# Symmetric attention scores of layers 2 and 3: computed from the diagonal on, the rest by transposition

## The chip, the cores and the metric

The kernel runs on one core of a Trainium2 chip. The metric is the device time of one execution in microseconds (us), the median of several runs. Times within an execution come from the hardware profiler's trace of one of them.

## What is computed

The reference takes node features `x` (16 batches, 1024 nodes, 128 features) and a symmetric 0/1 adjacency matrix `adj` (16 x 1024 x 1024) with ones on its diagonal. Four graph layers follow each other, and each ends with `x = layernorm(x + layer(x))`. Layer 0 has batch norms over all batches. Layer 1 is an attention with additive scores. Layers 2 and 3, which the change touches, have this form; since `adj` is 0 or 1, only `a_0` counts:

```python
def scores(a):
    return leaky_relu(einsum('bnd,bmd->bnm', h * a, h), negative_slope=0.2)
alpha = full(adj.shape, -9e15)
for k, a in enumerate((a_0, a_1, a_2, a_3)):
    alpha = where(adj == k + 1, scores(a), alpha)
alpha = softmax(alpha, axis=-1)
return einsum('bnm,bmd->bnd', alpha, h)
```

The score of nodes n and m is the sum over d of `a[d] * h[n, d] * h[m, d]`, so the score matrix is symmetric, and so is the masked one, as `adj` is symmetric.

## The kernel before

Everything below is in `fast_path`; a `general_path` stands behind it for inputs that fail some tests, and these do not take it. A first part, up to about 390 us, does layer 0 over all batches, since its batch norms need sums over all of them. The rest, which the change touches, does layers 1 to 3 batch by batch. P is 128, N is 1024, D is 128, C = N / P = 8 row chunks, H = G = 2 halves of 512 columns, and A is D + 1.

A `Batch` object has one method for each stage. `weights` (L862) makes row chunk c (128 rows, 1024 columns) of the score matrix of layer 2 or 3. Two matmuls (L867) of 512 columns each, with the chunk of `xw` (the transposed features times `a_0`) as the stationary operand and `xt` (the transposed features) as the moving one, fill a PSUM tile `pbig` of two banks. VectorE subtracts a penalty `pen` from it, which is large where there is no edge (L870), and applies the leaky relu (L871). ScalarE takes the exponential in place (L872). The result is `e`, one tile of 8 x 1024 columns for each layer, with one buffer.

`sum` (L874) multiplies `e` with the features of the layer's input, to which a column of ones is joined, so that the column D of the product is the softmax's denominator. For an output chunk c it runs over m: the stationary operand is the block `e[:, m, c*P:(c+1)*P]`, that is row chunk m and column chunk c (L880), and the product accumulates in a PSUM tile `pacc` that holds up to three output chunks. Three such calls make a layer's sums. VectorE then divides, adds the residual (L888) and collects the layer norm's moments (L722, L723). `apply` (L742) ends the layer norm on ScalarE.

Other stages of a batch: `transpose` (L757 to L761) makes `xt` and `xw`; `residual0` does layer 0's last step (L777, L784, L786, L789); `scores1` (L804 to L806) makes two exponentials of one row for layer 1; `chunk1` does layer 1's row chunks (penalty L827, a comparison of `adj` with its transpose from the diagonal on L835, weights L838 and L841, matmuls into `po` L848). The PSUM tiles come from three pools of eight banks together: `r_big` with 2 buffers of two banks, `r_sum` with one of two banks, `r_acc` with 2 of one bank. Operands in fp32 are multiplied in two passes, so a matmul shows as two instructions in the trace; a transpose shows as one.

The order of the work is written out by hand. `place` (L927) gives each step of a stage a position: a whole number for the turn, plus a fraction that runs from a first to a last value over the stage's steps. In one turn t four batches are in work: layer 1 of batch t, layer 2 of t - 1, layer 3's scores of t - 2 and its sums of t - 3:

```python
for t in range(-1, B + 3):
    place(t, 0.04, 0.92, t, layer1)
    place(t, 0.08, 0.50, t - 1, scores, 2, V_L2)
    place(t, 0.54, 0.94, t - 1, sums_of, 2)
    place(t, 0.54, 0.98, t - 2, scores, 3, V_L3)
    place(t, 0.02, 0.42, t - 3, sums_of, 3)
    place(t, 0.30, 0.80, t + 1, residual0)
for _, f in sorted(order, key=lambda o: o[0]):
    f()
```

The sorted list is the order in which the steps are written down. The tile framework adds the waits and the choice of buffers. It keeps the list's order roughly: in the trace a sum's first matmuls stand between matmuls of scores that are later in the list. Each engine then works its own queue in order.

Of the kernel before, what the change touches and what calls it, by code (L numbers as in the profile page):

```python
# [8 lines left out]
F32 = mybir.dt.float32  # L9
I32 = mybir.dt.int32  # L10
U8 = mybir.dt.uint8
AF = mybir.ActivationFunctionType
ALU = mybir.AluOpType
# [3 lines left out]
P = 128  # L17
# [373 lines left out]
def fast_path(ctx, tc, x, adj, adjt, k1, k2, w1, vecs, b_w, b_a, out, bad):  # L391
# [311 lines left out]

    with tc.tile_pool(name="r_load", bufs=3) as loads, tc.tile_pool(name="r_rows", bufs=2) as rows, \
            tc.tile_pool(name="r_work", bufs=1) as work, \
            tc.tile_pool(name="r_big", bufs=2, space=PSUM) as ps_big, \
            tc.tile_pool(name="r_sum", bufs=1, space=PSUM) as ps_sum, \
            tc.tile_pool(name="r_acc", bufs=2, space=PSUM) as ps_acc:

        class Norm:  # L710

# [33 lines left out]
        class Batch:  # L745
# [51 lines left out]
            def scores1(self):  # L797
                self.pen = rows.tile([P, C, N], FP8, name="pen", bufs=3)
                self.u1 = work.tile([P, N], F32, name="u1")
                self.u2 = work.tile([P, N], F32, name="u2")  # L800
                pu = ps_big.tile([P, N], F32, name="pbig")
                for h in range(H):
                    cols = slice(h * 512, (h + 1) * 512)
                    nc.tensor.matmul(pu[:, cols], wa1_rep, self.xt[:, cols], start=True, stop=True)  # L804
                nc.scalar.activation(self.u1, pu, AF.Exp, bias=c1_rep[:, 0:1])
                nc.scalar.activation(self.u2, pu, AF.Exp, bias=c1_rep[:, 1:2], scale=SLOPE)  # L806

            def values1(self):
                self.hn = work.tile([P, C, A], F32, name="hn")
# [51 lines left out]
            def weights(self, c, layer, v0):  # L861
                if c == 0:  # L862
                    self.e = work.tile([P, C, N], F32, name=f"e{layer}_")
                ps = ps_big.tile([P, N], F32, name="pbig")
                for h in range(H):
                    cols = slice(h * 512, (h + 1) * 512)
                    nc.tensor.matmul(ps[:, cols], self.xw[:, c * P:(c + 1) * P], self.xt[:, cols],  # L867
                                     start=True, stop=True)
                e = self.e[:, c, :]
                nc.vector.tensor_tensor(e, ps, self.pen[:, c, :], ALU.subtract)  # L870
                nc.vector.scalar_tensor_tensor(e, e, SLOPE, e, ALU.mult, ALU.max)  # L871
                nc.scalar.activation(e, e, AF.Exp, bias=shifts[v0])  # L872

            def sum(self, c0, n, xl, layer):  # L874
                norm = self.norm
# [20 lines left out]
        def does(f, *a):  # L896
            return lambda: f(*a)
# [12 lines left out]
        def scores(s, layer, v0):  # L910
            def begin():
# [2 lines left out]
                             for g in range(G)],  # L914
                    *[does(s.weights, c, layer, v0) for c in range(C)]]

        def sums_of(s, layer):
            def begin():
                s.norm = Norm(layer)
            return [begin, *[lambda c=c: s.sum(c, min(3, C - c), s.xin, layer)  # L920
                             for c in range(0, C, 3)],
                    lambda: s.norm.apply()] + ([s.store] if layer == 3 else [])
# [4 lines left out]
        def place(t, a, z, b, steps, *args):  # L927

            if 0 <= b < B:
                s = steps(at_work.setdefault(b, Batch(b)), *args)  # L930
                order.extend((t + a + (z - a) * k / len(s), f) for k, f in enumerate(s))


        for t in range(-1, B + 3):
            place(t, 0.04, 0.92, t, layer1)
            place(t, 0.08, 0.50, t - 1, scores, 2, V_L2)
            place(t, 0.54, 0.94, t - 1, sums_of, 2)
            place(t, 0.54, 0.98, t - 2, scores, 3, V_L3)
            place(t, 0.02, 0.42, t - 3, sums_of, 3)
            place(t, 0.30, 0.80, t + 1, residual0)  # L940
        for _, f in sorted(order, key=lambda o: o[0]):
            f()
# [78 lines left out]
```

## Time and profile before

| | |
|---|---|
| time, median of 3 runs | 1962.81 us (1955.96 to 1966.09) |
| span of the profiled execution | 1967.1 us |
| TensorE, matmuls | busy 1735.1 us, 88% |
| VectorE | busy 1540.6 us, 78% |
| ScalarE | busy 997.4 us, 51% |
| GpSimd | busy 148.1 us, 8% |
| DMA | 216.40 MB, mean 110 GB/s |

In the profile PE is TensorE's matmuls, PEld its loads of the stationary operand, DVE VectorE, ACT ScalarE and POOL GpSimd. The page cuts the span into 40 equal slices of 49.2 us and gives for each the busy share of an engine in tenths. A row of the groups of instructions names line, engine, operation, what is written from what, shape and count; after the bar stand the busy time of the group in us, the mean duration of one in ns, and the idle time of the engine just before them with what ended it. The table of windows gives busy times in stretches of the span. The list of waits tells who waited for whom: us in total, how often, and the longest. The chain is the work that ended last, followed back from the end. Matmuls are pipelined, so that the durations of neighbours overlap.

### The profile page before, as it was taken

Reading aid. Unit: us, or ns where it says so; the run is one execution under the profiler, and the core shown is the slowest. Engines: PE = TensorE matmul, PEld = TensorE weight load, DVE = VectorE, ACT = ScalarE, POOL = GpSimd, SP = SyncE. Lnnn points to the kernel's source line nnn. Section 1 sums busy time; section 2 is a strip of 40 time slices with the busy share of each in tenths; the row PEclk is TensorE's granted clock in tenths of the full one; section 3 lists DMA queues with packets and bytes.
Section 4 is the critical chain, followed back from the end, with each engine's and each line's share of the span. In section 5 each row is a group of like instructions: output and inputs, shape, how many; then the busy total and the mean of one; then the engine's idle time right before and its main releaser. Section 6 shows DMA issues by size and latency. Waiting matters only on the chain.

```text
span 1967.1 us, 26476 instructions
## 1 busy us (share of the span) xinstructions
PE 1735.1 (88%) x9453; PEld 1258.0 (64%) x9453; DVE 1540.6 (78%) x3803; ACT 997.4 (51%) x1809; POOL 148.1 (8%) x252
## 2 busy tenths in 40 slices
PE   6989999767889999999989998999999999999895
PEld 6988889633556565656656656666565656566574
DVE  4655555477697989897989798988989798979764
ACT  4544444245445555556464655556554555555532
POOL 0000000010101000101011010101010100000100
PEclk9999999889899999999999999999999999999998
DMA  8966664352340405041413232322314140402000
GB/s 297 326 235 244 225 215 162 116 156 69 108 127 28 146 20 154 24 144 29 138 57 110 66 101 70 109 75 92 103 64 133 34 142 25 140 17 62 12 1 24
DMA packets 110959, 216.40 MB, mean 110 GB/s; under 512 B 7776, under 2 KB 63712, under 8 KB 110816
## 3 DMA queue, kind: packets, MB, share of 16 engines
q1 hardware_dynamic: 108512, 206.08, 32.1%
q10 hardware_dynamic: 2304, 8.52, 1.1%
q8 instruction: 76, 1.25, 0.3%
q14 instruction: 67, 0.55, 0.1%
HBM read 197.67 MB, written 16.91 MB: 109 GB/s over the span
## 4 chain that ended last, share of the span: by engine, by line
PE 41%; DVE 35%; ACT 8%; DMA 7%; issue 4%; POOL 4%; SPq 0%; DVEq 0%; ACTq 0%
PE pacc L880 17%; PE pbig L867 6%; DVE e L838 5%; PE po L848 5%; DMA at<-in_adj_dram 5%; PE pb L543 5%; DVE e L841 5%; PE pz L506 3%; DVE ln_st L722 1%; DVE e L835 1%; ACT m L499 1%; POOL rs_t L442 1%; PE pacc L757 1%; DVE hn L817 1%; PE moments L536 1%
## 5 line engine op out<-in xcount | busy, mean ns | idle before, releaser
L848 PE MATMUL po<-e,hn 128*128 128x512 f32 x512 | 249.0, 615 | 14.5 <-ACT hn L845 14.3
L827 ACT ACTIVATE pen<-adjt,minus_root 128x1024 fp8e5<-128x1024 int32 x128 | 146.5, 1147 | 82.3 <-DMA adjt<-in_adjt_dram 82.0
L543 PE MATMUL pb<-v,m 128*128 128x258 f32 x1024 | 156.8, 295 | 24.2 <-DVE g L548 23.8
L848 PEld LDWEIGHTS po<-e,hn 128*128 128x128 f32 x512 | 93.9, 193 | 130.0 <-issue 81.6
L506 PE MATMUL pz<-x,m 128*128 128x258 f32 x1024 | 163.6, 301 | 6.0 <-ACT m L499 3.3
L838 DVE SCALAR_TENSOR_TENSOR e<-u,q,u 128x1024 f32<-128x1024 f32 x128 | 161.5, 1272 | 0.3 <-ACT q L820 0.3
L543 PEld LDWEIGHTS pb<-v,m 128*128 128x128 f32 x1024 | 138.6, 198 | 28.8 <-DVE g L548 26.2
L841 DVE SCALAR_TENSOR_TENSOR e<-e,adjt 128x1024 f32<-128x1024 f32 x128 | 154.6, 1217 | 0.0
L506 PEld LDWEIGHTS pz<-x,m 128*128 128x128 f32 x1024 | 140.4, 199 | 8.7 <-ACT m L499 4.6
L884 DVE TENSOR_SCALAR sums<-pacc 128x3 f32<-128x3 f32 (+1 forms) x96 | 14.6, 152 | 146.6 <-PE pacc L880 146.6
L845 ACT ACTIVATE hn<-hn,rs 128x128 f32<-128x128 f32 x128 | 49.9, 398 | 115.2 <-DVE rs L844 92.1
L835 DVE SCALAR_TENSOR_TENSOR e<-adjn,adjt 128x1024 f32<-128x1024 int32 (+7 forms) x128 | 95.2, 745 | 4.8 <-PE po L848 3.1
L548 DVE TENSOR_TENSOR g<-pb,lo 128x129 f32<-128x129 f32 x128 | 36.0, 289 | 77.7 <-ACT lo L547 77.4
L499 ACT CAST m<-at 128x1024 fp32r<-128x1024 int32 x64 | 66.0, 1049 | 46.3 <-DMA at<-in_adj_dram 46.1
L509 DVE TENSOR_TENSOR z<-pz,lo 128x128 f32<-128x128 f32 x128 | 35.6, 287 | 65.4 <-ACT lo L508 65.0
L547 ACT COPY lo<-pb 128x129 f32<-128x129 f32 x128 | 33.1, 268 | 70.1 <-PE pb L543 68.1
L508 ACT COPY lo<-pz 128x129 f32<-128x129 f32 x128 | 33.1, 269 | 65.6 <-PE pz L506 65.5
L501 DVE CAST m<-at 128x1024 fp32r<-128x1024 int32 x64 | 43.9, 687 | 19.0 <-DMA at<-in_adj_dram 19.0
L536 PE MATMUL moments<-reg 128*128 128x130 f32 x256 | 48.9, 279 | 0.1
L551 PE MATMUL moments<-g 128*128 128x130 f32 x256 | 48.4, 274 | 0.0
L536 PEld LDWEIGHTS moments<-reg 128*128 128x128 f32 x256 | 39.0, 194 | 0.4 <-issue 0.3
L817 DVE TENSOR_TENSOR hn<-pacc,bw_row 128x387 f32<-128x387 f32 (+1 forms) x48 | 23.0, 502 | 20.7 <-PE pacc L815 20.4
(1169 smaller groups left out, 4266.3 us busy)
## 6 DMA issues: line engine op xcount, KB each, us to landing
at<-in_adj_dram SPq DMA_DIRECT2D x128, 512.0 KB, 5.6
adjt<-in_adjt_dram SPq DMA_DIRECT2D x128, 512.0 KB, 3.6
people<-g ACTq DMA_DIRECT2D x16, 520.0 KB, 7.1
g<-people SPq DMA_DIRECT2D x16, 520.0 KB, 4.6
xf<-in_x_dram SPq DMA_DIRECT2D x16, 512.0 KB, 4.1
adjn<-in_adj_dram SPq DMA_DIRECT2D x16, 512.0 KB, 4.2
x<-in_x_dram SPq DMA_DIRECT2D x16, 512.0 KB, 4.4
adjn<-in_adj_dram SPq DMA_DIRECT2D x16, 448.0 KB, 4.2
```

What stands on the lines that cost most here:

```text
L499: nc.scalar.copy(self.m[:, i, :], at)
L506: nc.tensor.matmul(pz[:, :2 * A], self.m[:, i, c * P:(c + 1) * P], self.x2[:, i, :], start=(i == 0), stop=(i == C - 1))
L536: nc.tensor.matmul(moments1[:, :A + 1], self.reg[:, c, :D], self.reg[:, c, :], start=(self.b == 0 and c == 0), stop=(self.b == B - 1 and c ...
L543: nc.tensor.matmul(pz[:, :2 * A], self.m[:, j, c * P:(c + 1) * P], self.v2[:, j].rearrange("p s a -> p (s a)"), start=(j == 0), stop=(j == ...
L827: nc.scalar.activation(self.pen[:, c, :], at, AF.Square, bias=minus_root, scale=BIG_ROOT, saturate=False, accum_out=checks[:, self.b, c:c ...
L835: nc.vector.scalar_tensor_tensor(e[:, :n], an[:, :n], 1.0, at[:, c * P:], ALU.mult, ALU.not_equal, accum_out=unlike[:, self.b, c:c + 1])
L838: nc.vector.scalar_tensor_tensor(e, self.u2, self.q[:, c:c + 1], self.u1, ALU.mult, ALU.max)
L841: nc.vector.scalar_tensor_tensor(e, e, 1.0, at, ALU.mult, ALU.mult, accum_out=total)
L845: nc.scalar.mul(self.hn[:, c, :D], self.hn[:, c, :D], rs)
L848: nc.tensor.matmul(self.po[:, cols], self.hn[:, c, :D], e[:, cols], start=(c == 0), stop=(c == C - 1))
L867: nc.tensor.matmul(ps[:, cols], self.xw[:, c * P:(c + 1) * P], self.xt[:, cols], start=True, stop=True)
L880: nc.tensor.matmul(po[:, k, :], self.e[:, m, c * P:(c + 1) * P], xl[:, m, :], start=(m == 0), stop=(m == C - 1))
```

## The change

A chunk c of scores is computed only from its diagonal block on: columns c*P to N, in pieces of at most 512 columns, each in a PSUM tile of one bank. Leaky relu and exponential run over those columns alone. The blocks left of the diagonal come from the new stage `mirror`: the blocks of row chunk c right of the diagonal are transposed on TensorE, up to four into one bank of `r_acc`, and ScalarE copies them to their places in column chunk c. That makes 28 transposes and 10 copies for a layer and batch. The aim is to spare TensorE, VectorE and ScalarE the half of the matrix that is there already. The mirrors are placed in the order about a sixth of a turn behind the scores of their chunks, so that the exponentials have been done when the transposes come. The PSUM pools are cut anew: `r_big` has 3 buffers of one bank and `r_acc` 3 of one bank. `scores1` is fitted to the one-bank tiles, with four activations of 512 in place of two of 1024. The stages are shifted a little in the order.

```diff
-            tc.tile_pool(name="r_big", bufs=2, space=PSUM) as ps_big, \
+            tc.tile_pool(name="r_big", bufs=3, space=PSUM) as ps_big, \
...
-            tc.tile_pool(name="r_acc", bufs=2, space=PSUM) as ps_acc:
+            tc.tile_pool(name="r_acc", bufs=3, space=PSUM) as ps_acc:
...
-                pu = ps_big.tile([P, N], F32, name="pbig")
                 for h in range(H):
                     cols = slice(h * 512, (h + 1) * 512)
-                    nc.tensor.matmul(pu[:, cols], wa1_rep, self.xt[:, cols], start=True, stop=True)
-                nc.scalar.activation(self.u1, pu, AF.Exp, bias=c1_rep[:, 0:1])
-                nc.scalar.activation(self.u2, pu, AF.Exp, bias=c1_rep[:, 1:2], scale=SLOPE)
+                    pu = ps_big.tile([P, 512], F32, name="pbig")
+                    nc.tensor.matmul(pu, wa1_rep, self.xt[:, cols], start=True, stop=True)
+                    nc.scalar.activation(self.u1[:, cols], pu, AF.Exp, bias=c1_rep[:, 0:1])
+                    nc.scalar.activation(self.u2[:, cols], pu, AF.Exp, bias=c1_rep[:, 1:2],
+                                         scale=SLOPE)
...
-                ps = ps_big.tile([P, N], F32, name="pbig")
-                for h in range(H):
-                    cols = slice(h * 512, (h + 1) * 512)
-                    nc.tensor.matmul(ps[:, cols], self.xw[:, c * P:(c + 1) * P], self.xt[:, cols],
+                for a in range(c * P, N, 512):
+                    cols = slice(a, min(a + 512, N))
+                    n = cols.stop - cols.start
+                    ps = ps_big.tile([P, 512], F32, name="pbig")
+                    nc.tensor.matmul(ps[:, :n], self.xw[:, c * P:(c + 1) * P], self.xt[:, cols],
                                      start=True, stop=True)
-                e = self.e[:, c, :]
-                nc.vector.tensor_tensor(e, ps, self.pen[:, c, :], ALU.subtract)
+                    nc.vector.tensor_tensor(self.e[:, c, cols], ps[:, :n], self.pen[:, c, cols],
+                                            ALU.subtract)
+                e = self.e[:, c, c * P:]
                 nc.vector.scalar_tensor_tensor(e, e, SLOPE, e, ALU.mult, ALU.max)
                 nc.scalar.activation(e, e, AF.Exp, bias=shifts[v0])
+
+            def mirror(self, c):
+                for a in range(c + 1, C, 4):
+                    n = min(4, C - a)
+                    pt = ps_acc.tile([P, 4, P], F32, name="pacc")
+                    for k in range(n):
+                        nc.tensor.transpose(pt[:, k, :], self.e[:, c, (a + k) * P:(a + k + 1) * P],
+                                            ident)
+                    nc.scalar.copy(self.e[:, a:a + n, c * P:(c + 1) * P], pt[:, :n, :])
...
+        def mirrors(s):
+            return [does(s.mirror, c) for c in range(C - 1)]
...
-            place(t, 0.08, 0.50, t - 1, scores, 2, V_L2)
-            place(t, 0.54, 0.94, t - 1, sums_of, 2)
-            place(t, 0.54, 0.98, t - 2, scores, 3, V_L3)
-            place(t, 0.02, 0.42, t - 3, sums_of, 3)
+            place(t, 0.06, 0.44, t - 1, scores, 2, V_L2)
+            place(t, 0.24, 0.52, t - 1, mirrors)
+            place(t, 0.56, 0.94, t - 1, sums_of, 2)
+            place(t, 0.56, 0.94, t - 2, scores, 3, V_L3)
+            place(t, 0.74, 1.02, t - 2, mirrors)
+            place(t, 0.06, 0.44, t - 3, sums_of, 3)
```

## The prediction, made before the result was known

> **What bounds the kernel now.** I read the page's busy shares first.
>
> ```profile
> PE 1735.1 (88%) x9453; PEld 1258.0 (64%) x9453; DVE 1540.6 (78%) x3803; ACT 997.4 (51%) x1809; POOL 148.1 (8%) x252
> PE   6989999767889999999989998999999999999895
> DVE  4655555477697989897989798988989798979764
> PE 41%; DVE 35%; ACT 8%; DMA 7%; issue 4%; POOL 4%; SPq 0%; DVEq 0%; ACTq 0%
> ```
>
> Two engines share the end: TensorE leads slightly, VectorE alternates with it in the chain that ended last. From slice 9 on (390 us) layers 1 to 3 run. There the trace repeats. The timeline shows the same score matrix stage 92.8 us apart, and the table of windows 92.8 us long gives the same busy sums each time (columns: PE, PEld, DVE, ACT, POOL busy, instructions in brackets, granted clock, DMA share, GB/s):
>
> ```profile
> 1109.00:1201.80 92.80, 84.61 (x427) 56.48 (x427) 82.77 (x200) 52.22 (x89) 8.78 (x12) 0.98 0.28 88
> 1201.80:1294.60 92.80, 84.90 (x431) 56.53 (x430) 83.20 (x201) 52.05 (x89) 8.78 (x12) 0.98 0.28 89
> ...
> 1222.00:1235.00 13.00, 10.70 (x60) 7.30 (x58) 13.00 (x24) 6.12 (x8) 0.00 (x0) 1.00 0.27 84
> ...
> 1246.00:1258.30 12.30, 12.30 (x72) 8.67 (x71) 11.69 (x35) 7.89 (x14) 0.00 (x0) 1.00 0.20 75
> ...
> 1276.00:1288.30 12.30, 12.30 (x90) 11.36 (x91) 5.11 (x26) 7.53 (x12) 0.00 (x0) 0.90 0.08 23
> ```
>
> So a turn (one batch) costs 92.8 us, TensorE is busy 84.9 of it and VectorE 83.2. No third party is near: DMA 28%, ACT 52 us. The cut into stretches shows who rules where: 1222 to 1235 is VectorE without a gap while TensorE has some; 1276 to 1288 is TensorE without a gap while VectorE is idle for more than half. The change takes work from both. Last, what TensorE waits for in that turn (us in total, times, longest):
>
> ```profile
> PE pacc L880 <- ACT e__10360 L872: 3.1, 4, 2.2
> PE pacc L880 <- ACT e__10006 L872: 1.5, 1, 1.5
> PE pbig L867 <- DVE e__10006 L870: 1.4, 1, 1.4
> PE pacc L757 <- DVE xl__10105 L789: 0.7, 1, 0.7
> ```
>
> with two more of 0.5 and 0.4 us, so 7.6 us of waits, all ending at VectorE or at an exponential fed by VectorE.
>
> **What the skill says.** The Trainium skill, "TensorE: Matmul & The Clock Gate", Part 4: a transpose is a matmul against the identity, lands in PSUM and needs a copy after it; about 275 ns in one kernel. The trace agrees on the record (L757 280 ns), but these overlap: four in a run show as 0.60 us. "VectorE: DVE Perf Modes", the TRN2 errata: a fixed cost per instruction, (N+151)/0.96 ns for an fp32 tensor_tensor, so many small pieces pay it many times. It gives 691 ns at 512 and 1224 at 1024; the trace has 685 and 1216 (L835), so it holds. "Perfetto Trace Analysis", Identifying the Most-Contended Engine, warns that TensorE's busy share is no measure of its distance from its peak; I use it only as time that an unchanged group takes. The same page's Optimization Strategy takes a bubble that repeats as a sign of too few buffers; the 1.4 us of L867 behind L870 is one, once a turn.
>
> **The change, part by part.** Per layer and batch.
>
> Scores (L867). Now 16 matmuls of 512 columns, each two passes: 32 instructions. Runs of them in the timeline are 0.43 us apart (four take 1.88 with a 0.59 tail), so 32 x 0.43 = 13.8 us, 0.84 ns per column and pass. From the diagonal on, the widths are 1024, 896, ... 128, together 4,608 of 8,192 columns, in 12 pieces: 2 x 4,608 x 0.84 = 7.7 us. Saved 6.0, for two layers 12.0 us of TensorE a turn.
>
> Mirrors. 28 transposes a layer, of one pass like L757 and L777 (8 instructions for 8 blocks). Bounds: 0.11 us each as in a stream (seven of L777 end 0.93 us after the first starts), 0.165 as in a lone run of four that the chain charges with 0.66 us. I take 0.13: 28 x 0.13 = 3.6 us, 7.3 for two layers (6.2 to 9.2). TensorE net: -4.7 us a turn, to **80.2** (79.0 to 82.1).
>
> Subtraction and leaky relu (L870, L871), on VectorE. The trace happens to hold these very widths in L835, which is also triangular:
>
> ```profile
> L835 DVE SCALAR_TENSOR_TENSOR e<-adjn,adjt 128x1024 f32<-128x1024 int32 x1 | 1.2, 1216 | 0.0
> L835 DVE SCALAR_TENSOR_TENSOR e<-adjn,adjt 128x896 f32<-128x896 int32 x1 | 1.1, 1079 | 0.0
> L835 DVE SCALAR_TENSOR_TENSOR e<-adjn,adjt 128x512 f32<-128x512 int32 x1 | 0.7, 685 | 0.0
> ...
> L835 DVE SCALAR_TENSOR_TENSOR e<-adjn,adjt 128x384 f32<-128x384 int32 x1 | 0.5, 548 | 0.0
> L835 DVE SCALAR_TENSOR_TENSOR e<-adjn,adjt 128x256 f32<-128x256 int32 x1 | 0.4, 390 | 0.0
> L835 DVE SCALAR_TENSOR_TENSOR e<-adjn,adjt 128x128 f32<-128x128 int32 x1 | 0.3, 258 | 0.0
> ```
>
> With 948 at 768 and 817 at 640 the eight sum to 5.9 us; L871 has 8 x 1.21 = 9.7 now, so 3.8 saved. L870 comes in 12 pieces: six of 512, two each of 384, 256, 128: 6 x 0.685 + 2 x (0.548 + 0.390 + 0.258) = 6.5 against 9.7, so 3.2 saved. Two layers: 14.0 us, VectorE goes to **69** a turn.
>
> Exponentials and copies, on ACT. An exp of 1024 takes 1.14; taking 0.40 for 128 (L845) and a straight line between, the eight widths sum to about 6.2 against 9.1: saved 2.9. Ten copies out of PSUM a layer: four of 512 (0.58, L759), two of 384, of 256 and of 128 (0.27, like L508's 269 ns), with 0.47 and 0.37 between: 4.5. Net +1.6 a layer, +3.2 a turn. The split of L805/L806 into halves adds about 0.1 (two of 0.59 for one of 1.10). ACT goes from 52 to some 55.5 us, 65% of a turn of 85; hidden behind TensorE.
>
> Order and waits. New: a transpose waits for the exp of its row; behind it on TensorE stand scores, sums and layer 1's L848. A row's subtraction, relu and exp take 1.2 us each, about 5 us from L870 to the exp's end in the timeline (1199.67 to 1204.4). Mirrors stand 0.08 to 0.11 of a turn after their row in the list, 7 to 9 us of 85: enough in a steady turn, with 2 to 4 us to spare. The copy on ACT waits for the transposes; behind it stand exps, for which only sums and later mirrors wait. Sums of layer 3 start after 0.04 to 0.08 of a turn, but their first block needs only rows and mirrors 0 to 2, where it needed all eight rows before. That goes at the 4.6 us of L880 behind L872.
>
> Buffers. r_big holds three single banks for two double ones: TensorE may be three pieces, one and a half wide rows, ahead of VectorE instead of two rows. A piece takes 0.86 us of TensorE and 0.69 of VectorE, so VectorE is the faster side, but its queue also holds layer 1's 1.2 us instructions. This can cost a wait per wide row. r_acc has three banks for two; the mirrors use it besides the sums and transposes.
>
> **How it sums.** TensorE is now the one bound, at 80.2 us busy with VectorE at 69. Its idle time was 7.9 us a turn. VectorE, behind most of it, has 14 us more slack, while mirrors and smaller buffers add places to wait; I leave 4.8. The turn: 80.2 + 4.8 = 85.0, 7.8 less, times 16 batches = 125 us. The first 390 us and the drain are left as they are. 1963 - 125 = **1838**.
>
> **Rivals.**
> 1. TensorE without gaps. For: stretches as 1276 to 1288 have none, and VectorE's slack is large. Against: 7.6 us of named waits today. Turn 80.2, saving 12.6 x 16 = 202: 1761.
> 2. The mirrors' waits eat most. Twenty runs of transposes a turn, each between an exp and an ACT copy; at 0.3 us each (the size of the small waits L757 shows behind ACT, 0.2 to 0.6) 6 us more: turn 91, 1934. For: the margin of 2 to 4 us; against: TensorE's queue holds other ready work, the trace shows sums slipped in between scores.
> 3. Slower: the single banks bind. The bubble of L867 behind L870 was 1.4 us where VectorE was behind. If each of 24 pieces lost 0.45, a third of that, 10.8 us come on top of 85: turn 95.8, 1963 + 48 = 2011. For: the lookahead shrinks in columns from 2048 to 1536 and VectorE interleaves long instructions. Against: the narrower rows need one piece each, and the wait shows once a turn with 7 to 8 us of VectorE slack.
>
> **Chances and range.** 0.57 for the forecast (some 1795 to 1885), 0.19 for rival 1, 0.14 for rival 2, 0.10 for rival 3. Transposes at their dear end give 1868, at the cheap end 1819. The range 1770 to 1930 leaves out rival 3, about half of rival 2 and the last of rival 1. Faster by over 0.5% (under 1953): 0.86; within: 0.04; slower: 0.10.
>
> **What would show it.** Right: turns near 85 us; L867 at about 15.5 us and mirror transposes at 6 to 9 us of TensorE a turn; VectorE near 69 with idle time behind TensorE; TensorE the largest share of the chain by far. Wrong: L867 waiting for L870 many times a turn (rival 3); transposes waiting for L872, or sums for the mirror copies (rival 2); transposes apart by 0.2 us or more; ACT over 60 us a turn.

## The result, and the profile after

The changed kernel takes **1940.58 us** (median of 4 runs, 1933.93 to 1942.21), beside 1960.56 us for the kernel before on the same chip: a ratio of **0.9891**, 95% interval 0.9854 to 0.9927. So it is about 20 us faster, where 125 us had been forecast.

The page of the changed kernel, busy times, two rows of slices and the chain:

```profile
PE 1628.1 (84%) x10093; PEld 1298.2 (67%) x10093; DVE 1321.6 (68%) x3931; ACT 1027.7 (53%) x2161; POOL 138.2 (7%) x252
...
PE   6999999767888888797888888888888888888795
...
DVE  4655555477696959595968677686868595858444
...
PE 57%; DVE 15%; ACT 13%; DMA 9%; POOL 3%; issue 2%; SPq 0%; DVEq 0%; ACTq 0%
```

The work did go: VectorE is busy 219 us less than before, TensorE 107 us less. But TensorE is now below nine tenths in nearly every slice of the steady part (from slice 9 on), where it was mostly at nine or more before. If one engine were now the bound, it would be full; here both have less to do in nearly the same time. In the chain, ScalarE has risen from 8% to 13%.

I measure a turn from layer 1's first output activation of one batch (`u` from `po`, L856) to that of the next. Over the 11 middle turns it is 93.5 us before and 93.0 after, nothing like the 7.8 us forecast. What was gained lies mostly in the first three turns of the pipeline, while it fills: 70.3, 78.6 and 96.5 us before, 62.7, 67.5 and 92.8 after. That is 22.4 us of the 29.2 between the spans of the two profiled executions (1967.1 and 1937.9 us).

The table of windows of the changed kernel, one turn, then three stretches of it (columns as in the prediction: PE, PEld, DVE, ACT, POOL busy, granted clock, DMA share, GB/s):

```profile
1257.30:1349.40 92.10, 78.75 (x466) 59.74 (x465) 69.50 (x208) 53.45 (x110) 7.99 (x12) 0.93 0.27 89
1257.30:1267.50 10.20, 10.20 (x70) 8.09 (x69) 4.78 (x14) 4.42 (x7) 0.00 (x0) 1.00 0.01 2
...
1324.00:1336.00 12.00, 11.37 (x80) 9.26 (x78) 11.80 (x47) 6.12 (x11) 1.46 (x4) 1.00 0.03 9
1336.00:1349.40 13.40, 6.02 (x31) 5.57 (x32) 2.15 (x8) 12.55 (x30) 2.62 (x3) 0.62 0.00 1
```

TensorE's 78.75 us and VectorE's 69.50 are what the prediction had counted (80.2 and 69). What is off is the rest: TensorE stands idle for 13.4 us of the turn. The last line shows where over half of that lies. From 1336.0 to 1349.4 TensorE is busy for 6.0 us and VectorE for 2.2, while ScalarE works almost without a gap. VectorE stands still from the turn's end into the head of the next one, as its list of waits has, below TensorE's (us in total, times, longest). The last line is of the kernel before, for the turn from 1201.8 to 1294.6:

```profile
PE pacc L882 <- ACT e__12004 L875: 8.0, 2, 5.1
PE po L849 <- ACT hn L846: 4.5, 1, 4.5
PE pacc L784 <- ACT xw__11912 L761: 0.8, 1, 0.8
DVE sums L896 <- PE pacc L892: 17.3, 4, 13.4
...
DVE sums L884 <- PE pacc L880: 7.0, 2, 3.9
```

TensorE's three waits, 13.3 us together, are its whole idle time in the turn. The mirrors of layer 3 (L882) wait 8.0 us for the last exponentials of their layer; before, the largest such sum for one tile was 3.1 us. VectorE waits up to 13.4 us on end for the sums (L892), where its whole wait for sums was 7.0 us a turn. This wait ran from 1247.2 to 1260.6, so 10 us of it lie in the end of the turn before: TensorE was itself still waiting for an exponential until 1251.0, then it did transposes and 6.8 us of sums. TensorE's timeline at the seam of two turns, changed kernel (start, duration, line, operation, count; in brackets the idle time ahead of it and who ended it):

```profile
1338.28 0.69 PE L882 MATMUL pacc<-ident,e__12004 128*128 128x128 f32 x2 [2.92 <-ACT e__12004 L875]
1344.07 0.47 PE L882 MATMUL pacc<-ident,e__12004 128*128 128x128 f32 x1 [5.09 <-ACT e__12004 L875]
1344.33 1.06 PE L757 MATMUL pacc<-ident,xl__11718 128*128 128x128 f32 x4
...
1346.89 3.31 PE L892 MATMUL pacc<-xl__11111,e__12004 128*128 128x129 f32 x21
```

ScalarE's timeline, the same kernel, shows what that time went into, and one earlier line that matters:

```profile
1310.70 3.19 ACT L742 ACTIVATE xl__11718<-xl__11718,ln_off__12071,ln_rstd__12067 128x128 f32<-128x128 f32 x8 [2.44 <-DVE ln_off__12071 L740]
...
1337.63 0.60 ACT L875 ACTIVATE e__12004<-e__12004,shift 128x384 f32<-128x384 f32 x1
1338.14 2.40 ACT L742 ACTIVATE xl__11893<-xl__11893,ln_off__12211,ln_rstd__12207 128x128 f32<-128x128 f32 x6
1340.45 3.17 ACT L742 ACTIVATE xl__12024<-xl__12024,ln_off__12225,ln_rstd__12221 128x128 f32<-128x128 f32 x8
1343.52 0.79 ACT L875 ACTIVATE e__12004<-e__12004,shift 128x256 f32<-128x256 f32 x2
```

The last two exponentials (L875) stand in ScalarE's queue behind layer norms (L742), so the mirror at 1344.07 has to wait. ScalarE is not the only one that is late. VectorE's timeline of the same rows:

```profile
1338.83 0.17 DVE L740 SCALAR_TENSOR_TENSOR ln_off__12225<-ln_mv__12026,ln_rstd__12221 128x8 f32<-128x8 f32 x1 [1.53 <-POOL ln_rstd__12221 L443]
1338.91 0.61 DVE L871 TENSOR_TENSOR e__12004<-pbig,pen 128x256 f32<-128x256 f32 x2
1339.44 0.62 DVE L874 SCALAR_TENSOR_TENSOR e__12004<-e__12004 128x256 f32<-128x256 f32 x2
```

The matmuls of these scores had ended by 1335.4. Their subtraction (L871) stood on VectorE behind a step of the layer norm (L740), which itself waited for GpSimd, and the leaky relu (L874) ended at 1340.1. So the norms on ScalarE kept the exponentials back for the last 3.5 us, from 1340.1 to 1343.5; what went before was lost on VectorE and GpSimd.

The wait alone would be harmless if TensorE had other work in the meantime. It had: `xl__11718`, which the transposes of the next turn (L757) read, was finished at 1313.9, 30 us before they ran. In the kernel before, the same place of TensorE's timeline reads otherwise:

```profile
1258.50 3.60 PE L867 MATMUL pbig<-xt__10252,xw__10253 128*128 128x512 f32 x8
1261.93 0.60 PE L757 MATMUL pacc<-ident,xl__10105 128*128 128x128 f32 x4
1262.37 0.83 PE L880 MATMUL pacc<-xl__9552,e__10360 128*128 128x129 f32 x6
...
1264.47 1.98 PE L867 MATMUL pbig<-xt__10252,xw__10253 128*128 128x512 f32 x4
```

There the next turn's transposes and layer 3's first sums (L880) run between scores. So two questions came out of the comparison: is it the wait for the exponentials that costs, and why does the ready work stand behind it?

### The profile page after: what moved, and what is told of

Same layout as the page of the kernel before. It is cut to its first block, busy times and chain, and to the rows that moved or that the text cites. A ratio compares the mean times of both kernels' runs of the same rounds, so it can differ in the third digit from the quotient of the medians.

```text
span 1937.9 us, 28354 instructions
## 1 busy us (share of the span) xinstructions
PE 1628.1 (84%) x10093; PEld 1298.2 (67%) x10093; DVE 1321.6 (68%) x3931; ACT 1027.7 (53%) x2161; POOL 138.2 (7%) x252
## 4 chain that ended last, share of the span: by engine, by line
PE 57%; DVE 15%; ACT 13%; DMA 9%; POOL 3%; issue 2%; SPq 0%; DVEq 0%; ACTq 0%
PE pacc L892 21%; PE pbig L869 8%; PE po L849 8%; PE pb L543 5%; DMA at<-in_adj_dram 5%; DMA adjt<-in_adjt_dram 4%; PE pz L506 4%; PE pacc L757 3%; DVE e L839 2%; PE pacc L882 2%; PE pbig L804 2%; PE pacc L816 1%; DVE ln_st L722 1%; ACT m L499 1%; DVE e L842 1%
## 5 line engine op out<-in xcount | busy, mean ns | idle before, releaser
L849 PE MATMUL po<-e,hn 128*128 128x512 f32 x512 | 267.4, 654 | 82.2 <-ACT hn L846 82.2
L849 PEld LDWEIGHTS po<-e,hn 128*128 128x128 f32 x512 | 96.4, 204 | 191.8 <-ACT hn L846 110.7
L543 PE MATMUL pb<-v,m 128*128 128x258 f32 x1024 | 155.6, 294 | 22.8 <-DVE g L548 22.4
L846 ACT ACTIVATE hn<-hn,rs 128x128 f32<-128x128 f32 x128 | 50.9, 402 | 79.6 <-DVE rs L845 73.4
L551 PEld LDWEIGHTS moments<-g 128*128 128x128 f32 x256 | 39.0, 190 | 0.0
```

The source lines that it names most:

```text
L543: nc.tensor.matmul(pz[:, :2 * A], self.m[:, j, c * P:(c + 1) * P], self.v2[:, j].rearrange("p s a -> p (s a)"), start=(j == 0), stop=(j == ...
L551: nc.tensor.matmul(moments2[:, :A + 1], self.g[:, c, :D], self.g[:, c, :], start=(self.b == 0 and c == 0), stop=(self.b == B - 1 and c == ...
L849: nc.tensor.matmul(self.po[:, cols], self.hn[:, c, :D], e[:, cols], start=(c == 0), stop=(c == C - 1))
```

## The experiments

Each ratio is against the kernel before, on the same chip, with its 95% interval. "Turn" is the mean of the 11 middle turns.

**Theory 1: late exponentials on ScalarE.** Three edits test it: take the wait away, give it time, take the norms out of ScalarE's way.

`e1_ones`, transposes of a constant in place of the exponentials:

```diff
-  nc.tensor.transpose(pt[:, k, :], self.e[:, c, (a + k) * P:(a + k + 1) * P], ident)
+  nc.tensor.transpose(pt[:, k, :], ones, ident)
```

> All 56 transposes a turn and their copies stay, but they transpose a constant tile of ones in place of the exponentials, so no transpose waits for an exponential (the left half of the attention matrix is then ones; the output is not the reference's). Theory (TensorE's queue stands behind the last transposes of layer 3, whose exponentials stand on ScalarE behind two layer norms; the clock then falls to half): the 8.0 us of waits of the transposes and most of the half-clock stretch after them (up to 5 us) go, the turn falls from 92.1 to 80 to 84 us, the time to 1750 to 1815 us. Rival A (the added transposes and copies cost this as work): nothing changes, 1920 to 1950 us.

Measured: 1865.7 us, 0.9508 (0.9486 to 0.9531), turn 88.3. The same instructions without the wait bring 75 us, so the wait costs; but neither the range expected here nor the forecast turn of 85 is reached. Mirrors that wait for nothing hold nothing back either, so this run can't tell the wait itself from what stands behind it. The list of waits of this kernel, one turn:

```profile
PE po L849 <- ACT hn L846: 4.5, 1, 4.5
PE pacc L757 <- ACT xl__8896 L742: 2.9, 1, 2.9
```

The wait at the turn's end has only been passed to the next transposes (L757), which now stand behind another layer norm.

`e3_late3`, layer 3's mirrors and sums later:

```diff
-            place(t, 0.74, 1.02, t - 2, mirrors)
-            place(t, 0.06, 0.44, t - 3, sums_of, 3)
+            place(t, 0.86, 1.14, t - 2, mirrors)
+            place(t, 0.18, 0.56, t - 3, sums_of, 3)
```

> The mirrors and sums of layer 3 stand 0.12 of a turn later in the order (mirrors 0.86 to 1.14, sums 0.18 to 0.56). Theory: TensorE finds the next turn's transposes and scores ahead of the last mirrors, the wait of 8 us falls to under 3 and the half-clock stretch goes with it: 1800 to 1880 us. Rival A or B: within 1% of 1940 us.

Measured: 1881.28 us, 0.9596 (0.9575 to 0.9617), turn 88.8. That is 1 us outside the range expected. The placement was too tight for layer 3: in the change a mirror stands 0.08 to 0.11 of a turn behind the scores of its chunk (the sixth of a turn given with the change is the distance between the first steps of the two stages, and scores begin with transposes). Here it is 0.20 to 0.23. Relaxing it brings about 59 us, and again the turn stops near 88 to 89.

`e8_late3_apply2`, the same, and layer 2's norm put at 0.10 of the next turn, away from the last exponentials (layer 2's sums, a step fewer, move slightly with it):

```diff
-            ... lambda: s.norm.apply()] + ([s.store] if layer == 3 else [])
+            ... *([lambda: s.norm.apply(), s.store] if layer == 3 else [])]
...
+            place(t, 1.10, 1.10, t - 1, lambda s: [lambda: s.norm.apply()])
```

> The late mirrors and sums of layer 3 (1881 us), and besides layer 2's layer norm at 0.10 of the next turn, where its reader stands at 0.595, so that at the end of the turn ScalarE has eight layer norm instructions ahead of the next turn's first transposes in place of sixteen. Theory: TensorE's 3.0 us of wait for L742 at the turn's start go, 1835 to 1870 us. Rival E (VectorE's queue, not ScalarE's, sets when the last rows are done): 1870 to 1890 us.

Measured: 1860.2 us, 0.9495 (0.9448 to 0.9542), turn 87.7. Another 21 us, as expected.

`e4_dve_apply`, the layer norms (L742) on VectorE instead of ScalarE:

```diff
-  nc.scalar.activation(self.xl[:, c, :D], self.xl[:, c, :D], AF.Identity,
-                       bias=off[:, c:c + 1], scale=rstd[:, c:c + 1])
+  nc.vector.tensor_scalar(self.xl[:, c, :D], self.xl[:, c, :D], rstd[:, c:c + 1],
+                          off[:, c:c + 1], ALU.mult, ALU.add)
```

> The 32 layer norm instructions a turn (L742) run on VectorE in place of ScalarE. ScalarE loses 12.6 us a turn, VectorE gains about 7 (32 of some 0.2 us) and stands near 77 of 92. Theory: nothing stands any more between the last scores and their exponentials on ScalarE, both long waits of TensorE (8.0 us behind L875, 4.5 behind L846) shrink to under 4 together: 1780 to 1850 us. Rival A or B: ScalarE was only 58% busy, so nothing or a little slower, 1930 to 1970 us.

Measured: 1931.26 us, 0.9856 (0.9826 to 0.9887): a miss, inside the range of the rivals. The mirrors still wait, by this kernel's list over four turns:

```profile
PE pacc L882 <- ACT e__9658 L875: 7.2, 2, 4.3
PE pacc L882 <- ACT e__8876 L875: 7.1, 2, 4.3
```

Its VectorE timeline shows a block of eight norms (2.1 us) between the subtraction and the leaky relu of a last row: the queue ahead of the last exponentials has moved, not gone. So theory 1 names a real wait, but it doesn't say why the wait can't be filled.

**Which part of the change costs?** `e5_only2` and `e6_only3` mirror one layer only and compute the other in full rows:

```diff
+                first = c * P if layer == 2 else 0        # e6: layer == 3
-                for a in range(c * P, N, 512):
+                for a in range(first, N, 512):
...
-            place(t, 0.74, 1.02, t - 2, mirrors)          # e6: the other one
```

> Only layer 2 is mirrored; layer 3 has full score rows, in the new pools. Theory (the harm is where layer 3's last rows and mirrors meet the layer norms at the end of the turn; layer 2's mirrors stand amid other work): better than the kernel with no mirrors (1904 us): 1850 to 1890 us. Rival C (every mirror costs more than the half matrix saves): above 1904, about 1922 us, halfway to the full change.

Measured: 1924.36 us, 0.9839 (0.9805 to 0.9874), turn 92.1. A miss for the view that layer 2's part is sound by itself: its mirrors cost 20 us against the new pools without any mirror (`e2_none`, below, 1904). The rival that was given, that every mirror costs more than the half matrix saves, has it right at 1922.

> Only layer 3 is mirrored, layer 2 has full rows. Theory: worse than no mirrors, 1920 to 1960 us, with the long wait of L882 behind L875 at the end of the turn still there. Rival C: 1922 us as with layer 2 alone.

Measured: 1948.93 us, 0.9948 (0.9935 to 0.996), turn 93.9. As the theory expected, it is worse than no mirrors. The mirrors of layer 3 wait 8.8 us on end for their exponentials, once in each turn.

`e2_none` has the change's pools, pieces and places, but full rows and no mirrors:

```diff
-                for a in range(c * P, N, 512):
+                for a in range(0, N, 512):
...
-                e = self.e[:, c, c * P:]
+                e = self.e[:, c, :]
...
-            place(t, 0.24, 0.52, t - 1, mirrors)
-            place(t, 0.74, 1.02, t - 2, mirrors)
```

> Only the new PSUM pools, the one-bank pieces and the shifted order; full score rows, no mirrors. Theory: the pools cost nothing, since L869 waits for VectorE nowhere in the turn looked at; the time is that of the kernel before within 1.5%, 1935 to 1990 us. Rival B (the single banks eat the gain): 2000 us or more.

Measured: 1904.47 us, 0.9709 (0.9688 to 0.973), turn 90.5: a miss. Without any saving of work the kernel is 56 us faster than before, and 36 us faster than with the mirrors. Something beside the mirrors helps, and in these pools and places they cost more than they save. `e12_none_old_order` has also the places of the kernel before, and `e13_none_old_acc2`, on top of that, gives the third bank of `r_acc` back to `r_big`:

```diff
-            place(t, 0.06, 0.44, t - 1, scores, 2, V_L2)
+            place(t, 0.08, 0.50, t - 1, scores, 2, V_L2)
-            place(t, 0.56, 0.94, t - 1, sums_of, 2)
+            place(t, 0.54, 0.94, t - 1, sums_of, 2)
-            place(t, 0.56, 0.94, t - 2, scores, 3, V_L3)
+            place(t, 0.54, 0.98, t - 2, scores, 3, V_L3)
-            place(t, 0.06, 0.44, t - 3, sums_of, 3)
+            place(t, 0.02, 0.42, t - 3, sums_of, 3)
```

```diff
-            tc.tile_pool(name="r_big", bufs=3, space=PSUM) as ps_big, \
-            tc.tile_pool(name="r_acc", bufs=3, space=PSUM) as ps_acc:
+            tc.tile_pool(name="r_big", bufs=4, space=PSUM) as ps_big, \
+            tc.tile_pool(name="r_acc", bufs=2, space=PSUM) as ps_acc:
```

> The kernel with no mirrors and the new pools, in the order of the kernel before (scores 2 at 0.08 to 0.50, sums 2 from 0.54, scores 3 at 0.54 to 0.98, sums 3 at 0.02 to 0.42). If the one-bank pieces and the third r_acc bank made the gain of 55 us of the run without mirrors: 1895 to 1915 us. If the shifted order made it: 1945 to 1965 us.

> No mirrors, old order, one-bank pieces, but r_acc has 2 banks as in the kernel before and r_big 4. If the third r_acc bank makes the gain (1859 against 1961): 1930 to 1965 us. If the pieces make it: 1855 to 1885 us.

Measured: `e12_none_old_order` 1858.52 us, 0.9476 (0.9443 to 0.9509), turn 87.2; `e13_none_old_acc2` 1981.01 us, 1.0102 (1.0077 to 1.0128), turn 95.4. The first lies below both of its ranges: the shifted places had not helped but cost 46 us. The second lies above the upper of its ranges; the third bank makes more than the whole gain, as the pieces alone lose. The windows of four turns, first of `e12_none_old_order`:

```profile
900.00:1248.80 348.80, 333.89 (x1713) 220.43 (x1712) 335.33 (x865) 207.12 (x365) 34.83 (x48) 1.00 0.30 94
```

then of `e13_none_old_acc2`:

```profile
900.00:1281.60 381.60, 340.83 (x1717) 230.94 (x1717) 335.99 (x864) 209.86 (x365) 34.89 (x48) 0.97 0.28 86
```

The same work of VectorE (335 us) fills 96% of the four turns with three banks in `r_acc` and 88% with two. So one bank for sums and transposes, taken from four single ones of `r_big`, is worth 122 us. No line of the kernel before names such a shortage, but its page has a sign of it: VectorE's idle time before the first step behind the sums. The row of the kernel before, then that of `e12_none_old_order`:

```profile
L884 DVE TENSOR_SCALAR sums<-pacc 128x3 f32<-128x3 f32 (+1 forms) x96 | 14.6, 152 | 146.6 <-PE pacc L880 146.6
L896 DVE TENSOR_SCALAR sums<-pacc 128x3 f32<-128x3 f32 (+1 forms) x96 | 14.3, 149 | 53.6 <-PE pacc L892 53.5
```

VectorE's waits for sums over the four turns say the same, first `e12_none_old_order`:

```profile
DVE sums L896 <- PE pacc L892: 7.1, 8, 1.5
```

then `e13_none_old_acc2`:

```profile
DVE sums L896 <- PE pacc L892: 35.7, 12, 6.0
```

**A side question, the clock.** The records of the changed kernel show the granted clock halved for 10.24 us in most turns around this seam, and for 3.41 us elsewhere. `e7_warm` puts two groups of four matmuls, whose product is never read, ahead of layer 3's last mirrors:

```diff
+        def warm(s):
+            def fill():
+                pt = ps_acc.tile([P, 512], F32, name="pacc")
+                for _ in range(4):
+                    nc.tensor.matmul(pt, ones, s.xt[:, :512], start=True, stop=True)
+            return [fill, fill]
...
+            place(t, 0.937, 1.009, t - 2, warm)
```

> The change with two times four added matmuls on constants (of 512 columns, two passes, 3.4 us each four) ahead of layer 3's last two mirrors, in the two gaps of 2.9 and 5.1 us; nothing reads them. Theory: they lie in the gaps, and the clock no longer falls to half for 10 us after them: the turn is 3 to 5 us shorter, 1860 to 1895 us, though 6.9 us of TensorE work a turn are added. Rival D (the half clock costs nothing here, since the wait is ScalarE's): the same 1940 us or up to 15 us more.

Measured: 1928.58 us, 0.9854 (0.9819 to 0.9889), turn 92.1: a miss. The clock rises from 0.93 to 0.97 over four turns, and the turn falls by 0.9 us. The half clock lies in part over time in which TensorE waits anyway. The 0.9 us are what is left of the gain after the added matmuls, whose tiles also take banks of `r_acc`; what the half clock costs by itself this run doesn't show.

**Theory 2: mirrors that wait hold the banks of `r_acc`.** By this theory sums, transposes of the next turn and mirrors take their banks from one pool in the order of the list. The list has layer 3's last mirror at 0.98 of a turn, and only then the next turn's first transposes at 0.04 and the layer's first sums at 0.12. A mirror claims the next bank, then waits for its exponential; what comes after it in the list gets a bank only later, and its matmuls are put behind it in TensorE's queue, however ready they are. `e9_own_bank` gives the mirrors a bank of their own, at the price of one of `r_acc`; `e10_own_acc3` takes it from `r_big` instead:

```diff
# e9
-            tc.tile_pool(name="r_acc", bufs=3, space=PSUM) as ps_acc:
+            tc.tile_pool(name="r_acc", bufs=2, space=PSUM) as ps_acc, \
+            tc.tile_pool(name="r_mir", bufs=1, space=PSUM) as ps_mir:
...
-                    pt = ps_acc.tile([P, 4, P], F32, name="pacc")
+                    pt = ps_mir.tile([P, 4, P], F32, name="pmir")
# e10: r_acc bufs=3, and
-            tc.tile_pool(name="r_big", bufs=3, space=PSUM) as ps_big, \
+            tc.tile_pool(name="r_big", bufs=2, space=PSUM) as ps_big, \
```

> The change with a PSUM bank of its own for the mirrors (r_acc 2 banks, a new pool 1 bank, r_big 3). Theory, sharpened: in the change the last mirrors of layer 3 hold or claim all three r_acc banks while they wait for their exponentials, so the next turn's transposes (their input is ready 30 us before) and layer 3's first sums, which need such a bank too, cannot be put ahead of them in TensorE's queue; with a bank of their own they can. Waits of the mirrors' transposes fall from 8.0 to under 4 us a turn, 1870 to 1905 us. Rival E (VectorE's late last rows set the turn's end whatever TensorE does meanwhile): 1925 to 1945 us.

Measured: 1957.75 us, 0.9981 (0.9969 to 0.9993), turn 95.4: a miss. Among the longest waits none is of a mirror for its exponential any more; with one bank they wait for ScalarE's copies (L885), and the next turn's transposes for a layer norm. Over four turns:

```profile
PE pmir L883 <- ACT e__8433 L885: 4.1, 2, 3.2
...
PE pacc L758 <- ACT xl__11245 L743: 2.9, 1, 2.9
```

> As before, but r_acc keeps 3 banks and r_big has 2. If the r_acc banks matter more than score pieces ahead: better than the run with r_acc 2, 1850 to 1890 us. If the scores need their three banks: TensorE waits for VectorE at the score matmuls, 1900 to 1950 us.

Measured: 1831.7 us, 0.9336 (0.9305 to 0.9367), turn 87.2, better than either range. With three banks left for sums and transposes, the bank apart is worth 109 us against the change (1940.6). `e10_own_acc3` differs from `e9_own_bank` by that third bank and one of `r_big`; with two single banks TensorE waits some 3.6 us a turn for VectorE to free them, and the run is still 126 us faster. Its timelines at the seam, TensorE's and then ScalarE's, with the list of the change untouched:

```profile
1025.37 2.40 PE L893 MATMUL pacc<-xl__8768,e__9661 128*128 128x129 f32 x20
1027.60 0.27 PE L883 MATMUL pmir<-ident,e__9661 128*128 128x128 f32 x1
1027.71 2.84 PE L893 MATMUL pacc<-xl__8768,e__9661 128*128 128x129 f32 x24
```

```profile
1022.69 3.18 ACT L743 ACTIVATE xl__9681<-xl__9681,ln_off__9882,ln_rstd__9878 128x128 f32<-128x128 f32 x8
1025.77 0.79 ACT L876 ACTIVATE e__9661<-e__9661,shift 128x256 f32<-128x256 f32 x2
```

The last exponentials (L876) stand behind the eight norms (L743) as before. But TensorE no longer waits for them: it does the layer's first sums (L893) ahead of the last mirror (L883). So it is the place of the ready work that changed, not the lateness of the exponentials.

`e11_own_late3_apply2` is `e8_late3_apply2` with the pools of `e9_own_bank`, on top of its two edits:

```diff
-            tc.tile_pool(name="r_acc", bufs=3, space=PSUM) as ps_acc:
+            tc.tile_pool(name="r_acc", bufs=2, space=PSUM) as ps_acc, \
+            tc.tile_pool(name="r_mir", bufs=1, space=PSUM) as ps_mir:
```

> Late mirrors and sums of layer 3, layer 2's norm in the next turn, and the mirrors' own bank (r_acc 2). Theory: the late order already takes the last mirrors out of the way, so the own bank adds little and the lost r_acc bank costs a little: 1845 to 1880 us against 1860 without it.

Measured: 1897.74 us, 0.9646 (0.9608 to 0.9683): a miss, 37 us slower than without. That fits the loss of the third bank, though here no run with three took place.

Is it the bank apart, or just one more bank? `e14_acc4` has the sizes of `e10_own_acc3`, four banks beside two of `r_big`, but all four in `r_acc`:

```diff
-            tc.tile_pool(name="r_big", bufs=3, space=PSUM) as ps_big, \
-            tc.tile_pool(name="r_acc", bufs=3, space=PSUM) as ps_acc:
+            tc.tile_pool(name="r_big", bufs=2, space=PSUM) as ps_big, \
+            tc.tile_pool(name="r_acc", bufs=4, space=PSUM) as ps_acc:
```

> The change with r_acc 4 banks, shared by mirrors and all others, and r_big 2. If a bank more is what counts: as the run with the mirrors' own bank, 1825 to 1850 us. If a bank apart counts (waiting mirrors take whatever r_acc has): 1885 to 1940 us.

Measured: 1917.4 us, 0.9773 (0.9749 to 0.9797), turn 92.1, with this among the waits of four turns:

```profile
PE pacc L882 <- ACT e__9658 L875: 7.6, 3, 5.3
```

Same banks in number, same work, same places: shared 1917, apart 1832. Of the 109 us between the change and `e10_own_acc3`, 23 come with a fourth shared bank and 86 with its standing apart. The wait of the mirrors is there when they share and gone when they do not (in `e10_own_acc3` the largest is 1.0 us), and with the shared banks the seam reads as in the change: last mirror, transposes, then the first sums. This is the run that tells theory 2 from "too few banks".

Last, the places. `e15_after_old_order` is the change with the scores and sums placed as before (the mirrors stay where they are), `e16_own_acc3_old` adds to that the pools of `e10_own_acc3`. The places of both:

```diff
-            place(t, 0.06, 0.44, t - 1, scores, 2, V_L2)
-            place(t, 0.56, 0.94, t - 1, sums_of, 2)
-            place(t, 0.56, 0.94, t - 2, scores, 3, V_L3)
-            place(t, 0.06, 0.44, t - 3, sums_of, 3)
+            place(t, 0.08, 0.50, t - 1, scores, 2, V_L2)
+            place(t, 0.54, 0.94, t - 1, sums_of, 2)
+            place(t, 0.54, 0.98, t - 2, scores, 3, V_L3)
+            place(t, 0.02, 0.42, t - 3, sums_of, 3)
```

and the pools of `e16_own_acc3_old`:

```diff
+            tc.tile_pool(name="r_big", bufs=2, space=PSUM) as ps_big, \
...
+            tc.tile_pool(name="r_acc", bufs=3, space=PSUM) as ps_acc, \
+            tc.tile_pool(name="r_mir", bufs=1, space=PSUM) as ps_mir:
```

> The change with scores and sums at the places of the kernel before; mirrors, pools and pieces as in the change. If the shifted order costs with mirrors what it costs without (46 us): 1885 to 1905 us. If the waiting mirrors rule: 1930 to 1950 us.

Measured: 1924.21 us, 0.9812 (0.9769 to 0.9855), turn 93.2. That is in neither range, and the turn is that of the change (93.0); the 16 us between the two runs lie mostly in the first three turns (210.5 us together, against 223.0).

> Mirrors' own bank, r_acc 3, r_big 2, and the old places of scores and sums. If the two causes add up: 1785 to 1815 us. If TensorE's work (some 79 us of the turn) and the chain through ScalarE already bind in the run with the own bank (1832): 1820 to 1845 us.

Measured: **1704.69 us** (1702.62 to 1710.8), 0.8695 (0.8665 to 0.8724), turn 77.7. It is the best of all, 255 us faster than the kernel before on its chip (1959.7), with the same instructions as the change, and 80 us below the lower of its two ranges: that bank and places help each other so much was not foreseen. Page and one turn's window of `e16_own_acc3_old`:

```profile
PE 1573.7 (92%) x10093; PEld 1254.4 (74%) x10093; DVE 1304.8 (77%) x3931; ACT 1020.6 (60%) x2161; POOL 143.9 (8%) x252
```

```profile
1077.50:1155.00 77.50, 76.49 (x474) 57.83 (x473) 67.30 (x208) 53.63 (x112) 9.93 (x13) 1.00 0.35 111
```

The list of waits of that turn, TensorE's and VectorE's longest:

```profile
PE pacc L893 <- DVE xl__11478 L901: 0.5, 1, 0.5
PE pbig L870 <- DVE rs L845: 0.4, 1, 0.4
DVE sums L897 <- PE pacc L893: 6.1, 1, 6.1
```

and its TensorE timeline at the end of a layer's mirrors:

```profile
1132.97 0.49 PE L758 MATMUL pacc<-ident,xl__11237 128*128 128x128 f32 x3
1133.98 1.80 PE L893 MATMUL pacc<-xl__10310,e__11225 128*128 128x129 f32 x14 [0.52 <-DVE xl__11478 L901]
1135.62 0.38 PE L883 MATMUL pmir<-ident,e__11225 128*128 128x128 f32 x2
1135.83 0.83 PE L893 MATMUL pacc<-xl__10310,e__11225 128*128 128x129 f32 x6
...
1137.36 0.27 PE L883 MATMUL pmir<-ident,e__11225 128*128 128x128 f32 x1
```

The next turn's transposes (L758) and the sums of the very layer (L893) now stand ahead of the last mirrors and between them. TensorE is idle for 1.0 us of 77.5, and over four turns for 1.7 us a turn; it has become the bound that the prediction had wanted it to be.

## Why the prediction was wrong

**The work, right.** In the turn shown, the subtractions and leaky relus take 24.4 us of VectorE (L871 12.69, L874 11.72) against 38.6 before: 14.2 saved, 14.0 forecast. The exponentials take 12.2 against 18.1, saved 5.9, forecast 5.8. The mirror copies take 8.8 us of ScalarE, forecast 9.0. TensorE came to 78.75 (80.2 forecast), VectorE to 69.5 (69), ScalarE to 53.5 (55.5). TensorE's busy time is 76.0 a turn over four turns of `e16_own_acc3_old`, where its clock is whole; the same instructions take 79.1 a turn over four turns of the change, at 0.93.

**The idle time, wrong: "I leave 4.8".** TensorE's idle time went from 7.9 to 13.4 us a turn instead of down to 4.8. That is 8.6 us of the turn, against 1.4 that its work is below the forecast; 80.2 + 4.8 became 78.75 + 13.35. The forecast subtracted work from one engine's turn and supposed that gaps behind VectorE would shrink with VectorE's load. Here two engines alternate. At the turn's end TensorE waits for layer 3's exponentials, and VectorE with it; then TensorE does transposes and sums without a gap, and VectorE still waits for them, 13.4 us in all.

**"Enough in a steady turn, with 2 to 4 us to spare", wrong for layer 3.** This margin set the row's chain of some 5 us against its place in the list, and left out what is queued ahead of its steps. On ScalarE 5.6 us of layer norms (2.40 and 3.17) stand between two exponentials, of which 3.5 us held them back; on VectorE the last subtraction began 3.5 us after its matmuls had ended. The prediction named what is queued behind the waiting transpose on TensorE, and not what is queued ahead of what it waits for. Later mirrors (`e3_late3`) bring 59 us.

**"r_acc has three banks for two; the mirrors use it besides", the step that failed most.** It named the pool and gave it no time in either direction. With the change's one-bank pieces and the old places, the third bank alone brings 122 us (1981 to 1859), and mirrors that share the pool lose 66 (1859 to 1924), although they save work. So they undid half of what the bank had brought; the shifted places took 16 more (1924 to 1941), and the pieces with two banks in `r_acc` had cost 21 at the start (1960 to 1981). The saved work itself shows only when the mirrors have a bank apart: 1859 to 1705, 154 us, with the places of before. With the change's own places and a bank apart the time is 1832, close to the forecast of 1838, though with a turn of 87.2 and not 85.0. The rest comes from the fill (204.9 us for the first three turns, against 245.4), which the forecast had left as it was, so that nearness is luck. These differences are between medians from several chips, on which the kernel before took 1959.1 to 1961.6 us.

The prediction had read in "Perfetto Trace Analysis", Optimization Strategy, of the Trainium skill, that a bubble that repeats can mean too few buffers, and applied it to 1.4 us of L867 behind L870. The place where it held was `r_acc`, whose third bank was worth 122 us. Its shortage stands in no list of waits as such; it showed as VectorE waiting for sums, 146.6 us on the page of the kernel before, which the prediction did not use.

**The rivals.** Rival 2 had the size (turn 91, 1934) and the kind of cause, waits of the mirrors, but not the form: not twenty waits of 0.3 us at ScalarE's copies, but 8.0 us in two waits for exponentials and 4.5 us in one of layer 1 (L849 behind L846). "TensorE's queue holds other ready work", which spoke against it, was true of the work and untrue of the queue. Rival 3 did not come: none of TensorE's three waits in the turn of the change is for a score bank. Even two single banks for the scores are no bar: `e10_own_acc3` waits some 3.6 us a turn for them and `e16_own_acc3_old` 0.4 in the turn shown, and both are faster. The 21 us that the pieces cost in `e13_none_old_acc2` were not traced. Rival 1 (1761, no gaps) is what `e16_own_acc3_old` reached and passed, by other pools.

**Of the signs it listed:** L867's busy time fell by 12.5 us (30.9 to 18.4 as L869), where 12.0 had been forecast. VectorE went to 69, TensorE leads the chain by far (57 to 15%), and yet the turn did not move. "Transposes waiting for L872" was listed as a sign of being wrong, and is what came (L882 behind L875).

**What stays open.** Why the shifted places cost 16 us with shared banks, 46 without mirrors (1859 to 1904) and 127 with a bank apart (1705 to 1832) was not traced. That last is the largest unexplained figure of all. That the order of bank claims is what holds ready matmuls back is read from the timelines and fits `e10_own_acc3`, `e14_acc4` and `e16_own_acc3_old`; the claims themselves are in no trace. The 4.5 us of L849 behind L846 stay in `e1_ones` too and are gone in `e16_own_acc3_old`; they were not studied alone.

## What to carry to other kernels

Work taken from two engines that alternate is time saved only if ready work can move into the gap; ask of each new waiting step which buffers it claims, and which ready steps later in the list draw on the same pool. Try to give a step that waits its own PSUM bank, and choose the pool that pays for it: here the scores could spare one (1941 to 1832), the sums could not (1958). Look again at banks and places once the work has changed. To size a wait, count the queue ahead of what is waited for, not only the producer's own chain.

## What was not expected of the hardware

The transposes run 0.11 us apart at the full clock (seven in 0.93 us, the last of which takes 0.27) and 0.21 at half, as L757 shows in the seam (four in 1.06 us, against 0.60 in the kernel before). "TensorE: Matmul & The Clock Gate", Part 1, of the Trainium skill, has the clock halved after a window of some 3.4 us of idleness. The records agree roughly: a stretch of 10.24 us begins at the seam as the wait of 2.9 us ends, so somewhat earlier than a whole idle window would allow, and takes in the wait of 5.1 us; one of 3.41 us follows the wait of 4.5 us elsewhere in the turn. What was not expected is how little of that stretch costs time: of 10 us of half clock some 5 lie over a wait. In the rest the three groups of four transposes at the seam start 0.86 us apart, where four spaced by 0.11 would take 0.44, and the 48 instructions of sums behind them take 6.33 us against 5.52 for the next 48. From these figures the half clock at the seam costs an estimated 2 us a turn.
